# A state-space scan summed by accumulating DMA in SBUF, with three PSUM banks for the side work and one bank for the experts

## The chip, the cores and the metric

The kernel runs on one NeuronCore of a Trainium2 chip. The metric is the device time of one execution in microseconds, as the median of several runs. Everything is fp32; the attention scores use TensorE's fp32r form.

## The reference

Input `x` has 4 images of 128 channels and 64 x 64 pixels, that is L = 4096 tokens each. Two layers follow each other.

Layer 0 normalises, runs a 3 x 3 depthwise convolution with a GELU branch, and then a Mamba block on four groups of 32 channels. The part that matters here is the scan. It has 64 inner channels for each group and N = 16 states:

```
dA  = exp(delta[..., None] * A)                 # A is (64, 16)
dBu = delta[..., None] * Bm[:, :, None, :] * xin[..., None]
h_t = dA_t * h_(t-1) + dBu_t                    # for each channel and state
y_t = sum over n of h_t[:, n] * C_t[n]          # einsum 'bdn,bn->bd'
out = (y + D_skip * xin) * silu(z) @ out_proj_w.T
```

Layer 1 is attention with 4 heads of 32 over all 4096 tokens, softmax without a mask, and then a mixture of 8 experts of 128 x 128: a softmax router, the two largest probabilities renormalised, and `sum over k of p_k * (x @ W_e(k) + b_e(k))`.

## The kernel before, in words

The tokens of an image are cut into 8 blocks of 512. A block of the scan is split into two halves `p` (two of the four channel groups each, 2 x 64 channels = 128 partitions), and the 16 states into 8 pairs. A **unit** is (image b, block i, half p, state pair n): 4 x 8 x 2 x 8 = 512 units. A unit takes two **slots**, so the scan has 1024 slots (`END`). One Python loop over slots writes out all instructions; the `Queue` class makes each engine issue them in exactly that order (so nearly all carry the line of that helper, L467). Nothing reorders them later.

In a slot the loop puts out, in this order: transfers due (`flush`), the fetch of B or C rows for a later unit (`rows`, 512 KB, broadcast from DRAM on SP's queue, four buffers), one decay `da` of the next unit on ScalarE; in the even slot `driven` (h = B row x du) and `scan` on VectorE; in the odd slot `read` (hc = C row x h, 128 x 2 x 512: both states of the pair). One **attention group** goes with each slot when one is ready: two `sc` score tiles on TensorE, two exponentials `pT` on ScalarE, and, one slot later, the products `av` of the group before. Two **lanes**, X and Y, advance by two stages each in every slot. Lane Y makes the inputs of the scan: `first_norm`, `conv`, `inputs`. Lane X closes a block after its scan (`closed`) and does the output projection and experts of finished queries (`finished`), the latter also on lane Y after the scan has ended. Each `yield` in these functions ends a stage. `fetch` calls `until`, which forces the lanes on if a unit's inputs aren't ready.

The sum over the 16 states is on TensorE. Each 128 x 512 product `hc` is transposed in four pieces onto one PSUM bank, in the accumulating mode, for 16 states in turn (`turned_on`); ScalarE copies the bank to `yT`, TensorE turns it back (`turned_back`), and VectorE adds `D_skip * xin` and multiplies with the gate (`scanned`). The list `due` says in which slot a product is taken up, `closing` when a sum is finished. A finished sum also lets lane Y begin the `inputs` that wait for it.

PSUM has eight banks: four for `sc`, one for `av`, one for `y` and one for each lane (`work("X")`, `work("Y")`). The function `inputs` runs in lane Y but also uses lane X's bank, for the gate `pz` and for the B and C rows `pb`.

In `finished`, each pair of experts writes its own accumulation to the lane's bank, and VectorE adds the bank to `res`:

```
            if e:
                vector.tensor_add(res, res, ps)
            vector.tensor_mul(w, w, xf[:, None, :].to_broadcast([P, 2, BLK]))
            yield
            ps = work(lane)
            for u in range(2):
                mm(ps, ew[:, e + u, :], w[:, u, :], u == 0, u == 1)
```

The tile `taps` holds nine diagonal matrices for the convolution of image 0, which runs on TensorE (the other images' convolution runs on VectorE). It lies in the constant pool.

Of the kernel before, what the change touches and what calls it, by code (L numbers as in the profile page):

```python
# [9 lines left out]
F32 = mybir.dt.float32  # L10
# [7 lines left out]
P = 128  # L18
C = 128
# [17 lines left out]
def conv_mamba_attn_moe_kernel(ctx: ExitStack, tc: tile.TileContext, t: dict):  # L37
# [46 lines left out]

    taps = const.tile([P, 9, P], F32, name="taps")
    for k in range(9):
        nc.vector.tensor_scalar_mul(taps[:, k, :], ident, fc1w[:, k : k + 1])
# [385 lines left out]
    def mm(out, lhsT, rhs, start=True, stop=True):  # L473
        tensor.matmul(out, lhsT=lhsT, rhs=rhs, start=start, stop=stop)
# [24 lines left out]
    def pool(name, bufs=1, space=None):  # L499
        return main.enter_context(  # L500
            tc.tile_pool(name=name, bufs=bufs, **({} if space is None else {"space": space}))
        )

    mix, att, side = pool("mix"), pool("att"), pool("side")
    ps_sc, ps_av, ps_y = pool("ps_sc", 2, PSUM), pool("ps_av", 1, PSUM), pool("ps_y", 1, PSUM)
    ps_work = pool("ps_work", 1, PSUM)


    def work(lane, shape=None):
        return ps_work.tile(shape or [P, BLK], F32, tag=f"work{lane}", name=f"ps_{lane}")  # L510
# [132 lines left out]
    def conv(b, i):  # L643
# [4 lines left out]
        def tap(k):  # L648
            y0 = y0_rows(b, i, k // 3, k % 3)
            w = fc1w[:, k : k + 1]  # L650

            if b == 0:
                mm(hr, taps[:, k, :], y0, k == 0, k == 8)
# [59 lines left out]
    def inputs(b, i, p):  # L713
# [3 lines left out]
        while held:  # L717
            yield
            yield
        held.add("in")  # L720
        ps = work("Y")
        summed(ps, [(inxc[:, j, :], pairs[:, p, 2 * j : 2 * j + BLK]) for j in range(2)])
        pz = work("X")
# [8 lines left out]
        pb = work("X")  # L732
# [4 lines left out]
        held.clear()  # L737
# [75 lines left out]
    def read(h, w):  # L813
        hc = mix.tile([P, 2, BLK], F32, name="hc", bufs=2)
        vector.tensor_mul(hc, w, h[:, :, 0:BLK])
        return hc

    def scanned(b, i, p, y):
        xin, zs, delta, du, bcd = in_of.pop((b, i, p))
        vector.scalar_tensor_tensor(xin, xin, dsk, y, ALU.mult, ALU.add)  # L820
        vector.tensor_mul(zs, xin, zs)
        gated[b, i, p] = zs

    def turned_on(y, term, first, last):

        for j in range(NT):
            s = slice(j * P, (j + 1) * P)
            tensor.matmul(
                y[:, s], lhsT=term[:, s], rhs=ident, start=first and j == 0,
                stop=last and j == NT - 1, is_transpose=True,  # L830
            )
# [6 lines left out]

    def turned_back(b, i, p, yT):
        y = ps_y.tile([P, BLK], F32, name="y")  # L840
        for j in range(NT):
            tensor.transpose(y[:, j * P : (j + 1) * P], yT[:, j * P : (j + 1) * P], ident)
        return b, i, p, y
# [243 lines left out]
    def finished(b, qb, lane):  # L1087
# [73 lines left out]

# [23 lines left out]
        ps = work(lane)  # L1185
        mm(ps, eb8, prT[0:NE, :])
        yield
        res = tmp(lane, "res")
        vector.tensor_add(res, ps, xf)
# [3 lines left out]
        yield  # L1193
        for e in range(0, NE, 2):
# [12 lines left out]
        vector.tensor_add(res, res, ps)  # L1207
# [92 lines left out]
    END = 2 * len(units)  # L1300

# [18 lines left out]
    waiting, summing = None, None  # L1320

    while (
        slot < END or due or closing or summing or waiting or left or later or lanes["X"] or running
# [13 lines left out]
        if summing:  # L1337
            summed_up(*summing)
            summing = None
# [6 lines left out]
        if unit and odd:  # L1346
            hc = read(h, rows.pop((at, 1)))
            late = 2 * (unit[3] == 0)
            due.append((slot + 1 + late, unit, 0, hc[:, 0, :], False))
            due.append((slot + 2, unit, 1, hc[:, 1, :], ends(unit)))  # L1350
        advance("Y", False)
        while closing and closing[0][0] <= slot:
            summing = turned_back(*closing.popleft()[1:])
        while due and due[0][0] <= slot:
            _, (b, i, p, n), k, term, done_with = due.popleft()
            first = n == 0 and k == 0
            if first:
                y_of[b, i, p] = ps_y.tile([P, BLK], F32, name="y")
            turned_on(y_of[b, i, p], term, first, done_with)
            if done_with:  # L1360
                yT = mix.tile([P, BLK], F32, name="yT")
                scalar.copy(yT, y_of.pop((b, i, p)))
                closing.append((slot + 1, b, i, p, yT))
# [123 lines left out]
```

## Time and profile before

| | |
|---|---|
| runs shown | 5223.30, 5229.83, 5244.32 us; median 5229.83 us |
| profiled execution, own time | 5221.24 us |
| its span | 5219.4 us |
| PE, PEld busy | 4743.5 us (91%), 2300.7 us (44%) |
| DVE, ACT busy | 3834.5 us (73%), 3749.8 us (72%) |
| POOL busy | 423.5 us (8%) |
| bytes moved by DMA | 1131.62 MB, mean 217 GB/s |
| SP's queue | 1126.74 MB, 64.3% of 16 engines |
| last `hc` product starts | 4608.4 us |

PE is TensorE, PEld its weight loads, DVE VectorE, ACT ScalarE, POOL GpSimd, SP the queue that issues transfers. In the slices, one digit stands for 130.5 us and gives the busy share in tenths. In a row of the groups, the name before `<-` is written and those behind are read; then come the number of instructions, the busy time, the mean duration of one, and the idle time of the engine just before them with what ended it. The profile counts two matmuls for one fp32 call, and one for an fp32r score or a transpose.

### The profile page before, as it was taken

The numbers are of one execution on the slowest core, as the hardware profiler recorded it, in microseconds if no ns is written. First come the engines' busy times: TensorE is split into PE (matmuls) and PEld (weight loads), VectorE is DVE, ScalarE is ACT, GpSimd is POOL, SyncE is SP. The second block draws the span as 40 slices with busy tenths as digits, with TensorE's granted clock in tenths as the row PEclk, the third lists the DMA queues.
The fourth block names the chain that finished last, engine by engine and source line by source line (L and its number), as shares of the span: only waits on it lengthen the run. The fifth ranks groups of instructions, "written<-read, shape, count | busy, mean of one in ns | idle before, by whom it ended". The sixth has DMA issues, their size and how long they took to land.

```text
span 5219.4 us, 62693 instructions
## 1 busy us (share of the span) xinstructions
PE 4743.5 (91%) x20704; PEld 2300.7 (44%) x20704; DVE 3834.5 (73%) x5809; ACT 3749.8 (72%) x5701; POOL 423.5 (8%) x483
## 2 busy tenths in 40 slices
PE   4566898999999999899999999999999999999997
PEld 2333444444444444444444444444444444443443
DVE  4888767777788877888788877888788877751332
ACT  3456787788777777688887787788777787756543
POOL 1111101100000000001000000000000001000000
PEclk8677999999999999899999999999999999999998
DMA  3556667767776667767766667767766666754542
GB/s 96 188 186 202 206 215 247 232 231 238 244 231 218 227 227 243 238 232 246 260 230 231 224 223 230 262 227 259 259 236 227 215 230 226 263 181 153 184 134 72
DMA packets 451694, 1131.62 MB, mean 217 GB/s; under 512 B 51985, under 2 KB 135330, under 8 KB 451362
## 3 DMA queue, kind: packets, MB, share of 16 engines
q1 hardware_dynamic: 450194, 1126.74, 64.3%
q8 instruction: 166, 2.72, 0.2%
q14 instruction: 166, 1.36, 0.1%
q10 hardware_dynamic: 1168, 0.80, 0.1%
HBM read 967.12 MB, written 143.39 MB: 213 GB/s over the span
## 4 chain that ended last, share of the span: by engine, by line
PE 55%; DVE 18%; ACT 13%; DMA 6%; issue 5%; POOL 2%; SPq 1%; DVEq 0%; ACTq 0%; POOLq 0%
PE av L467 23%; PE sc L467 13%; PE ps_X L467 8%; DVE h L467 6%; PE ps_Y L467 5%; PE y L467 5%; ACT pT L467 4%; ACT L467 3%; DMA ks<-kd 2%; DVE hc L467 2%; ACT xt L467 1%; ACT e L467 1%; DMA rows<-bcd 1%; DVE stX L467 1%; POOL rsX L467 1%
## 5 line engine op out<-in xcount | busy, mean ns | idle before, releaser
L467 ACT ACTIVATE pT<-sc 128x1024 f32<-128x1024 f32 x2048 | 1984.8, 1023 | 940.1 <-PE sc L467 938.4
L467 PE MATMUL av<-pT,v 128*64 128x512 f32 x8192 | 1998.3, 609 | 12.4 <-DVE avs L467 12.4
L467 PE MATMUL sc<-qs,ks 128*128 128x512 f32 x4096 | 1296.1, 436 | 64.4 <-DMA ks<-kd 32.7
L467 DVE TENSOR_TENSOR_SCAN h<-da,state,h 128x1025 f32<-128x1025 f32 x512 | 1204.2, 2352 | 90.0 <-ACT h L467 56.2
L467 PEld LDWEIGHTS sc<-qs,ks 128*128 128x128 f32 x4096 | 701.3, 190 | 793.3 <-ACT pT L467 261.7
L467 PEld LDWEIGHTS av<-pT,v 128*64 128x64 f32 x8192 | 499.5, 137 | 844.4 <-issue 813.8
L467 ACT ACTIVATE da<-delta,amat 128x512 f32<-128x512 f32 x1024 | 743.0, 730 | 1.9
L467 PE MATMUL y<-ident,hc 128*128 128x128 f32 x4096 | 626.6, 284 | 64.9 <-DVE hc L467 64.9
L467 DVE TENSOR_TENSOR hc<-rows,h 128x1024 f32<-128x1024 f32 x512 | 624.2, 1219 | 16.1 <-PE y L467 5.9
L467 DVE TENSOR_TENSOR h<-rows,du 128x1024 f32<-128x1024 f32 x512 | 623.4, 1218 | 14.2 <-DMA rows<-bcd 13.7
L467 PEld LDWEIGHTS y<-ident,hc 128*128 128x128 f32 x4096 | 520.6, 147 | 235.7 <-issue 83.9
L467 ACT ACT_TABLE_LOAD x319 | 409.3, 1283 | 19.5 <-DVE zs L467 14.3
L467 POOL TENSOR_TENSOR rsX<-rsX,mhalf 128x4 f32<-128x4 f32 x92 | 203.8, 2216 | 2524.6 <-DVE rsX L467 2440.5
L467 POOL TENSOR_TENSOR rsY<-rsY,mhalf 128x4 f32<-128x4 f32 x100 | 130.4, 1304 | 2071.0 <-DVE shiftY L467 1560.3
L467 DVE TENSOR_TENSOR avs<-av,prev 128x512 f32<-128x512 f32 x96 | 66.1, 689 | 252.9 <-PE av L467 238.3
L467 PE MATMUL ps_X<-share,w_ew 128*128 128x512 f32 x432 | 215.5, 622 | 8.7 <-DVE share L467 8.5
L467 ACT ACTIVATE xt<-ps_Y,shiftY,rsY 128x128 f32<-128x128 f32 x380 | 143.8, 469 | 106.4 <-POOL shiftY L467 99.0
L467 DVE TENSOR_TENSOR share<-share,xf 128x1024 f32<-128x1024 f32 x128 | 155.9, 1218 | 15.6 <-DMA share<-sharesX 9.9
L467 ACT COPY state<-h 128x2 f32<-128x2 f32 x448 | 88.7, 198 | 93.5 <-DVE h L467 93.5
L467 DVE SCALAR_TENSOR_TENSOR cm<-y,w_fc1w,cm 128x512 f32<-128x512 f32 x192 | 142.8, 744 | 3.4
L467 PE MATMUL ps_Y<-pairs,inxc 128*128 128x512 f32 x256 | 129.2, 629 | 15.6 <-DMA pairs<-xn 10.3
L467 PEld LDWEIGHTS ps_X<-share,w_ew 128*128 128x128 f32 x432 | 73.6, 190 | 146.8 <-issue 98.5
(254 smaller groups left out, 3455.8 us busy)
## 6 DMA issues: line engine op xcount, KB each, us to landing
rows<-bcd SPq DMA_DIRECT2D x1024, 512.0 KB
ks<-kd SPq DMA_DIRECT2D x192, 512.0 KB
qs<-qd SPq DMA_DIRECT2D x161, 512.0 KB
share<-sharesX SPq DMA_DIRECT2D x108, 512.0 KB
v<-vd SPq DMA_DIRECT2D x192, 256.0 KB
ks<-kd SPq DMA_DIRECT2D x128, 256.0 KB
avd<-avs SPq DMA_DIRECT2D x96, 256.0 KB
prev<-avd SPq DMA_DIRECT2D x96, 256.0 KB
```

What stands on the lines that cost most here:

```text
L467: return lambda *args, **kw: queued(op(*args, **kw))
```

## The change

1. The two products of a unit are no longer transposed and summed on TensorE. The product of the first pair of states is written to a tile of its own, `sum` (128 x 2 x 512). Each of the other seven pairs is added to it by a transfer within SBUF with an accumulate, issued from GpSimd's queue: 7 x 64 = 448 transfers of 512 KB. VectorE adds the two halves of the tile at the end, in `scanned`. `turned_on`, `turned_back`, `yT` and their bank go.
2. The bank goes to a third work tag, `Z`, that `inputs` uses in place of lane X's bank for `pz` and `pb`. The set `held` is no longer asked.
3. In `finished`, the bias product and all eight experts are accumulated in one bank, and VectorE adds that to `xf` once. Two yields are added ahead of the transposes of `both`.
4. `taps` leaves the constant pool: eight of the nine matrices lie in a buffer of `share`, the ninth in one of `acc`, both used later by `finished`.
5. A finished sum is taken up four slots after the last transfer is issued.

```
-    taps = const.tile([P, 9, P], F32, name="taps")
-    for k in range(9):
-        nc.vector.tensor_scalar_mul(taps[:, k, :], ident, fc1w[:, k : k + 1])
...
-    ps_sc, ps_av, ps_y = pool("ps_sc", 2, PSUM), pool("ps_av", 1, PSUM), pool("ps_y", 1, PSUM)
+    ps_sc, ps_av = pool("ps_sc", 2, PSUM), pool("ps_av", 1, PSUM)
     ps_work = pool("ps_work", 1, PSUM)
+    tap8 = side.tile([P, 2, BLK], F32, name="share", bufs=3).rearrange("p k (j c) -> p (k j) c", c=P)
+    tap9 = side.tile([P, NT, C], F32, name="acc", bufs=2)[:, 0, :]
+    taps = [tap8[:, k, :] for k in range(8)] + [tap9]
+    for k in range(9):
+        vector.tensor_scalar_mul(taps[k], ident, fc1w[:, k : k + 1])
...
-        while held:
-            yield
-            yield
-        held.add("in")
         ps = work("Y")
         summed(ps, [(inxc[:, j, :], pairs[:, p, 2 * j : 2 * j + BLK]) for j in range(2)])
-        pz = work("X")
+        pz = work("Z")
...
-        pb = work("X")
+        pb = work("Z")
         mm(pb[0:DI, :], wbc, xin)
         ps = work("Y")
         mm(ps, wdt, xin)
         yield
-        held.clear()
...
-    def read(h, w):
-        hc = mix.tile([P, 2, BLK], F32, name="hc", bufs=2)
+    def read(unit, h, w):
+        hc = mix.tile([P, 2, BLK], F32, name="hc" if unit[3] else "sum", bufs=2)
         vector.tensor_mul(hc, w, h[:, :, 0:BLK])
         return hc
...
-        vector.scalar_tensor_tensor(xin, xin, dsk, y, ALU.mult, ALU.add)
+        vector.scalar_tensor_tensor(xin, xin, dsk, y[:, 0, :], ALU.mult, ALU.add)
+        vector.tensor_add(xin, xin, y[:, 1, :])
         vector.tensor_mul(zs, xin, zs)
...
(finished)
         yield
-
+        yield
+        yield
         ps = work(lane)
         for j in range(NT):
             tensor.transpose(ps[0 : 2 * NE, j * P : (j + 1) * P], both[:, j, :], ident)
...
-        ps = work(lane)
-        mm(ps, eb8, prT[0:NE, :])
-        yield
-        res = tmp(lane, "res")
-        vector.tensor_add(res, ps, xf)
+        yield
         yield
...
-            if e:
-                vector.tensor_add(res, res, ps)
             vector.tensor_mul(w, w, xf[:, None, :].to_broadcast([P, 2, BLK]))
             yield
-            ps = work(lane)
+            if e == 0:
+                ps = work(lane)
+                mm(ps, eb8, prT[0:NE, :], True, False)
             for u in range(2):
-                mm(ps, ew[:, e + u, :], w[:, u, :], u == 0, u == 1)
-        yield
-        vector.tensor_add(res, res, ps)
+                mm(ps, ew[:, e + u, :], w[:, u, :], False, e + u == NE - 1)
+        yield
+        res = tmp(lane, "res")
+        vector.tensor_add(res, ps, xf)
         send(out[b][:, s], res, 2)
...
(the loop over slots)
-        if summing:
-            summed_up(*summing)
-            summing = None
+        while closing and closing[0][0] <= slot:
+            summed_up(*closing.popleft()[1:])
         advance("X", True)
...
         if unit and odd:
-            hc = read(h, rows.pop((at, 1)))
-            late = 2 * (unit[3] == 0)
-            due.append((slot + 1 + late, unit, 0, hc[:, 0, :], False))
-            due.append((slot + 2, unit, 1, hc[:, 1, :], ends(unit)))
+            hc = read(unit, h, rows.pop((at, 1)))
+            if unit[3] == 0:
+                y_of[unit[:3]] = hc
+            else:
+                due.append((slot + 2, unit, hc))
         advance("Y", False)
-        while closing and closing[0][0] <= slot:
-            summing = turned_back(*closing.popleft()[1:])
         while due and due[0][0] <= slot:
-            _, (b, i, p, n), k, term, done_with = due.popleft()
...
+            _, (b, i, p, n), term = due.popleft()
+            gpsimd.dma_start(out=y_of[b, i, p], in_=term, accum_op=ALU.add)
+            if n == NST - 2:
+                closing.append((slot + 4, b, i, p, y_of.pop((b, i, p))))
         advance("Y", True)
```

More of the change, by code (lines that the diff above doesn't have):

```diff
@@ L652, in tap @@
             if b == 0:
-                mm(hr, taps[:, k, :], y0, k == 0, k == 8)
+                mm(hr, taps[k], y0, k == 0, k == 8)
             elif k == 0:
@@ L819, in scanned @@
         xin, zs, delta, du, bcd = in_of.pop((b, i, p))
-        vector.scalar_tensor_tensor(xin, xin, dsk, y, ALU.mult, ALU.add)
+        vector.scalar_tensor_tensor(xin, xin, dsk, y[:, 0, :], ALU.mult, ALU.add)
+        vector.tensor_add(xin, xin, y[:, 1, :])
         vector.tensor_mul(zs, xin, zs)
         gated[b, i, p] = zs
[L824 to L831, printed above, removed]
     def summed_up(b, i, p, y):
@@ L837, in summed_up @@
             lanes["X"].appendleft((("closed", b, i), closed(b, i), []))
[L839 to L843, printed above, removed]
     vst = side.tile([P, NH, NT, 2 * DH], F32, name="vst")
@@ L1193, in finished @@
         yield
+        ps = None
         for e in range(0, NE, 2):
@@ L1300, in conv_mamba_attn_moe_kernel @@
     END = 2 * len(units)
+    ALONE = NB // 2 * NST
     rows, due, closing, y_of = {}, deque(), deque(), {}
@@ L1318, in ends @@
         return unit[3] == NST - 2
-    waiting, summing = None, None
+    waiting = None
     while (
-        slot < END or due or closing or summing or waiting or left or later or lanes["X"] or running
+        slot < END or due or closing or waiting or left or later or lanes["X"] or running
     ):
@@ L1346, in conv_mamba_attn_moe_kernel @@
         if unit and odd:
-            hc = read(h, rows.pop((at, 1)))
-            late = 2 * (unit[3] == 0)
-            due.append((slot + 1 + late, unit, 0, hc[:, 0, :], False))
-            due.append((slot + 2, unit, 1, hc[:, 1, :], ends(unit)))
+            hc = read(unit, h, rows.pop((at, 1)))
[3 more added lines that the diff above has]
+                due.append((slot + 2, unit, hc))
         advance("Y", False)
-        while closing and closing[0][0] <= slot:
-            summing = turned_back(*closing.popleft()[1:])
         while due and due[0][0] <= slot:
-            _, (b, i, p, n), k, term, done_with = due.popleft()
[L1356 to L1363, printed above, removed]
+            _, (b, i, p, n), term = due.popleft()
+            gpsimd.dma_start(out=y_of[b, i, p], in_=term, accum_op=ALU.add)
+            if n == NST - 2:
+                closing.append((slot + 4, b, i, p, y_of.pop((b, i, p))))
         advance("Y", True)
```

## The prediction

> **What bounds the kernel now.** I read the forty slices first, then the windows, then the chain, then the groups. In the slices (busy tenths) TensorE stands at 9 from about 650 us to the end, VectorE and ScalarE at 7 and 8 until the scan ends at about 4620 us, the DMA engines at 6 and 7, GpSimd near nothing:
>
> ```profile
> PE   4566898999999999899999999999999999999997
> DVE  4888767777788877888788877888788877751332
> ACT  3456787788777777688887787788777787756543
> POOL 1111101100000000001000000000000001000000
> DMA  3556667767776667767766667767766666754542
> ```
>
> The windows turn that into time per slot of the scan. A slot issues four `y<-ident,hc` matmuls, so the number of those counts slots. First all instructions, then, in the second pair, only those on `hc`:
>
> ```profile
> 250.00:500.00 250.00, 156.07 (x593) 88.97 (x591) 213.68 (x274) 134.50 (x257) 28.36 (x28) 0.76 0.59 198
> 1000.00:4250.00 3250.00, 3089.35 (x13892) 1505.44 (x13889) 2634.68 (x3906) 2550.32 (x3907) 271.31 (x318) 0.99 0.70 236
> ...
> 250.00:500.00 250.00, 50.45 (x275) 42.05 (x273) 42.98 (x36) 0.76 0.59 198
> 1000.00:4250.00 3250.00, 420.68 (x2844) 348.98 (x2845) 433.82 (x356) 0.99 0.70 236
> ```
>
> Columns: length, busy time of PE, PEld, DVE, ACT and POOL, clock, DMA share, GB/s; the second pair has only PE, PEld and DVE. From 1000 to 4250 us there are 2844/4 = 711 slots, so **4.57 us a slot**, in which PE is busy 3089/711 = 4.35 us (95%), DVE 3.71 (81%), ACT 3.59 (78%), the DMA engines 0.70 x 4.57 = 3.20 us, moving 236 x 4.57 = 1.08 MB. TensorE sets the slot. The chain of waits agrees where nothing disturbs it: it runs through PE alone.
>
> ```profile
> 2544.48 0.44 PE y L467 x4
> 2544.91 1.87 PE av L467 x8
> 2546.78 1.13 PE sc L467 x4
> 2547.91 0.44 PE y L467 x4
> ```
>
> Of 1024 slots, 450/4 = 112 lie before 500 us (no attention yet, 3.64 us each in the second quarter millisecond, DVE 85% busy). The other **912** lie between 500 and 4620 us: this is the stretch that the change can shorten. From 4620 us on only attention and experts are left, with PE 93% busy; the scan's edits don't touch it.
>
> The groups that I price with (busy us, mean ns):
>
> ```profile
> L467 PE MATMUL y<-ident,hc 128*128 128x128 f32 x4096 | 626.6, 284 | 64.9 <-DVE hc L467 64.9
> L467 PE MATMUL y<-ident,yT 128*128 128x128 f32 x256 | 40.4, 282 | 2.7 <-ACT yT L467 2.7
> L467 ACT COPY yT<-y 128x512 f32<-128x512 f32 x64 | 37.9, 592 | 8.3 <-PE y L467 8.3
> L467 DVE TENSOR_TENSOR res<-res,ps_X 128x512 f32<-128x512 f32 x108 | 73.7, 682 | 51.9 <-PE ps_X L467 51.5
> L467 DVE TENSOR_TENSOR zs<-xin,zs 128x512 f32<-128x512 f32 x64 | 44.3, 692 | 2.2
> ```
>
> **What the Trainium skill says.** "DMA: Bandwidth & Descriptors", SWDGE vs HWDGE vs iDMA: accumulating in a transfer is for GpSimd's queue only, whose cores write the descriptors, and it runs on the same 16 engines as SP's transfers. Before has no such transfer; all its bulk traffic is on SP's queue at 64.3% of 16 engines. The same page, Rules for kernel authors: an accumulate reads its destination and writes it later, so each must wait for the one before on the same bytes. "Collectives: The Full Stack", The bandwidth ceiling: a reducing transfer reads two sources through the same read ring, and goes at half the rate of a copy; no run here shows it. "SBUF — State Buffer", SBUF: two separate sides: GpSimd can be locked out of its port while a DVE instruction holds it; the trace has a sign of that, `rsX` on POOL takes between 1007 and 2978 ns for 128x4.
>
> **The change, part by part.**
>
> *Sum over states: what goes.* 4096 + 256 PE matmuls, 626.6 + 40.4 = 667 us; in the middle 420.7/711 + 0.04 = 0.63 us a slot. PE falls from 4.35 to 3.72. ACT loses 64 copies, 38 us. PE also stops waiting for `hc` (64.9 us in all).
>
> *What the three engines would then allow.* PE 3.72, DVE 3.67 (below), ACT 3.55 are nearly equal. If PE keeps its idle time (4.57 - 4.35 = 0.22) the slot is 3.94; if DVE can't pass the 85% of the start, 3.67/0.85 = 4.32. I take **4.15**, between, and keep 3.94 to 4.32.
>
> *What comes: 448 transfers* (7 for each of 64 sums; the first pair of states is written in place), 7/16 = 0.4375 a slot, 512 KB each. Price P of one in time of all 16 engines: not in the trace. Floor: a copy at the page's ceiling of 435 GB/s, 1.2 us. Above: windows of 6 us in which the DMA share is 0.99 or more show 352 GB/s on average (63 of the 600 between 1000 and 4600 us, from 256 to 414); at that rate a copy takes 1.49 us, and two reads and a write one after another 4.5. I take two reads at 435, an estimate from the Collectives page: **P = 2.4**. The present 1.08 MB a slot at 352 GB/s need 3.06 us. Sum 3.06 + 0.4375 x 2.4 = 4.11 us; if the engines can be kept 95% busy, as PE is now, **4.33 us a slot**. That is more than 4.15: the DMA engines become the bound, and what they leave is 912 x (4.57 - 4.33) = **219 us**. The cover that hid the DMA (3.20 of 4.57) is almost used up.
>
> *The waits it brings.* On POOL each transfer waits for `hc` and for the transfer before it. Behind it stand the `rs` powers and shifts, for which ACT's `xt` waits (already 99.0 + 63.3 us). The transfers come every 16/7 slots, 9.9 us; an estimate is 8 us: about 1 to issue and 2 to land by the DMA page (Anatomy of one DMA), and 2.4 doubled because SP's packets take turns. So the wait is normally over. Descriptors on POOL: 448 x 0.5 to 3 us, against 424 us of work in 5219: covered by an idle engine. On DVE, `hc` must wait for the transfer two units back (four slots, 17 us: covered), and the sum is read four slots after the last transfer. SP issues nothing more, but its `rows` share the engines: they are issued some three slots ahead, 12 to 13 us, and wait now for only 13.7 us in all; this is the wait that I expect to grow.
>
> *The scan's end, two slots later.* Counted from a half-block's first slot, the sum was taken up at slot 19 and now at 21. Lane Y then has 24 slots of stages (3 inputs, 5 first norm, 13 conv, 3 inputs) and meets the fetch in slot 29: done in slot 28 instead of 26, still ahead. The three blocks with a group norm (7 slots more) overrun by two more slots; I put +5 us for forced stages, between 0 and 25.
>
> *DVE.* Experts: of 160 adds of about 686 ns 32 stay, -88 us. The second half of the sum: 64 adds like `zs`, +44 us. Net -44 us, 0.04 a slot, off the DMA-bound path: 0.
>
> *Third bank, later transposes.* PE waits in `ps_X` for `bothX` 45.9, `stX` 23.7, `lo` 20.3 and `zs` 13.8 us: at most -104 us, worth something only while PE sets the slot; with the DMA engines as the bound I count 0. The added two yields lengthen an experts' task by one slot: at most +4 us at the very end, against three to four adds less there: 0. Holding one bank for the whole sum costs nothing while a lane has one task.
>
> *Taps.* The same nine DVE instructions of 279 ns, moved behind the setup, in buffers that nobody else writes before 1366 us: 0, within 3 us either way.
>
> Sum against the profiled execution: 5221 - 219 + 5 = 5007 us. The median of the runs is 9 us above that execution; I forecast **5010**.
>
> **The rivals.**
>
> *Engines set the slot.* Accumulating costs little more than a copy (P under 1.9, where 3.06 + 0.83 over 0.95 is 4.1). For: the reads are from SBUF, and in single windows the DMA reached 414 GB/s. Against: two reads for each write. 5221 - 912 x 0.42 = 4840 us, with 3.94 even 4650.
>
> *The transfers cost more, and the DMA engines set a longer slot.* Place: the 16 engines in the 912 slots, seen as DVE waiting for `rows` and PE for `ks`. It decides from (4.57 x 0.95 - 3.06)/0.4375: **P = 2.93 us**. With P = 3.6, slot (3.06 + 1.58)/0.95 = 4.88: 5221 + 912 x 0.31 = 5504 us, slower. For: windows with the DMA share above 1 that moved only 294 GB/s, so a busy engine isn't a fast one. Against: SBUF reads don't go to HBM.
>
> *The transfers come too late after one another.* They are serial within a sum. It decides from a latency of 16 x 4.57/7 = 10.4 us; at 11 us a slot is 4.81: 5440 us. For: some transfers on the chain take that long (`total<-avs` 11.28 us at 2557 us, among others behind it in the queue). Against: most take about half (`ks<-kd` 5.87 us at 2527 us).
>
> *No change*, gain and loss cancel, P near 2.9: 5225 us.
>
> **How the numbers follow.** DMA engines just full, 5010: 0.33. Engines set the slot, 4840: 0.25. Costly transfers, 5504: 0.26. Late transfers, 5440: 0.09. No change: 0.07. The last counts as within 0.5% (26 us, about what a measurement of this kernel can tell from no change), the two before it as slower: faster 0.58, same 0.07, slower 0.35. The range takes in the engines' case down to a slot of 4.1 (4800) and the costly one up to P = 3.5 (5450). The likeliest case alone, P between 2.0 and 2.8, reaches from 4840 to 5170.
>
> **What would show it.** Right: no `y` group on PE, PE about 86% busy in the middle, a second DMA queue with some 235 MB, DMA share above 0.9 there, slots of 4.3 us, waits for `rows` and `ks` of some 100 us or more. The engines' case: DMA share under 0.85, `pT` and `sc` still the main waits. Costly transfers: the new queue's share over 25%, DMA share near 1, VectorE waiting for `rows`. Late transfers: DVE `hc` or POOL waiting for the accumulating transfer while the DMA share stays low. It would be wrong altogether if the slots before 500 us got longer by more than a tenth: then POOL or the serial chain is slow by itself, without any crowd.

## The result, and the profile after

| | before | after |
|---|---|---|
| runs, median | 5235.17 us (4 runs, 5223.30 to 5244.32; the table ahead of the prediction has three of them) | 5517.71 us (4 runs, 5502.07 to 5524.75) |
| profiled execution, own time, span | 5221.24, 5219.4 us | 5502.07, 5500.2 us |
| mean granted clock of TensorE | 0.958 | 0.900 |

The ratio is 1.0537, with a 95% interval from 1.0502 to 1.0572: the change makes the kernel **5.4% slower**. 5010 us was forecast, with a range up to 5450: it was to become faster, and became slower.

The slices of the kernel after (137.5 us each) and its two bulk queues:

```profile
PE   4344797888788898798888888888888888899997
DVE  4877767777677787877777777777677777751321
ACT  3445686777677777677677777677677777755553
POOL 1221212111111111111111111111121111110000
...
PEclk8566898999999899899999999899899999999998
DMA  3888889898888899999989889989988899974542
...
q1 hardware_dynamic: 450194, 1126.74, 59.8%
q0 software_dynamic: 64512, 234.91, 22.6%
```

TensorE (`PE`), at 9 in before from 650 us on, is at 8 until the scan ends; the DMA engines went from 6 and 7 to 8 and 9. The second queue (`q0`, GpSimd's) moves the expected 235 MB, and takes 22.6% of 16 engines for it, where SP's queue takes 59.8% for 1127 MB: by the byte the new traffic is 1.8 times as dear.

The windows; columns as in the prediction (length, busy time of PE, PEld, DVE, ACT and POOL, clock, DMA share, GB/s):

```profile
250.00:500.00 250.00, 103.83 (x244) 42.55 (x244) 199.44 (x256) 118.86 (x231) 53.40 (x54) 0.62 0.83 231
1000.00:4000.00 3000.00, 2552.60 (x9416) 1040.94 (x9415) 2269.61 (x3340) 2189.38 (x3335) 519.42 (x545) 0.92 0.90 270
```

The same with only the instructions on `rows`, on VectorE. There is one for each slot, so their number counts slots:

```profile
250.00:500.00 250.00, 76.31 (x64) 0.62 0.83 231
1000.00:4000.00 3000.00, 744.02 (x619) 0.92 0.90 270
```

From 1000 to 4000 us there are 619 slots: **4.85 us a slot** against 4.57 before and 4.33 forecast. In a slot PE is busy 4.12 us, DVE 3.67, the DMA engines 0.90 x 4.85 = 4.36.

The early slots, without attention, grew too. Counted the same way, before has 71 of these products in its second quarter millisecond:

```profile
250.00:500.00 250.00, 83.62 (x71) 0.76 0.59 198
```

That is 250/71 = 3.52 us a slot before and 250/64 = 3.91 after. (The 3.64 in the prediction counts transposes, and can't be set against it.) A count of so few is rough, so I also took the starts of VectorE's products `h`, all 512 of which are in both traces. The first 112 slots took 386 us before (98.1 to 483.7) and 419 after (97.6 to 517.0), 9% more; from there to the last `h` it is 4121 us before and 4367 after. The two stretches lost 34 and 246 us, 280 together, and the span grew by 281: the loss lies in the slots of the scan.

The chain that ended last, by engine and by line:

```profile
PE 32%; DMA 30%; DVE 19%; ACT 9%; issue 5%; POOL 2%; SPq 1%; DVEq 0%; POOLq 0%; ACTq 0%
PE av L463 14%; DMA sum<-hc 10%; PE sc L463 8%; DVE h L463 7%; DMA ks<-kd 5%; PE ps_X L463 5%; PE ps_Y L463 4%; DMA inv<-inverse 4%; DMA rows<-bcd 4%; ACT pT L463 3%; ACT L463 2%; DVE hc L463 2%; SPq L463 1%; ACT xt L463 1%; POOL rsX L463 1%
```

DMA is 30% of it, and `sum<-hc`, the new transfer, is its second entry. The groups (busy, mean ns | idle before, what ended most of it) and the DMA issue (KB, median us to landing):

```profile
L463 POOL DMA_DIRECT2D sum<-hc x448 | 395.9, 884 | 2444.6 <-DMA sum<-hc 1501.6
L463 DVE TENSOR_TENSOR hc<-rows,h 128x1024 f32<-128x1024 f32 x448 | 546.7, 1220 | 333.9 <-DMA sum<-hc 274.4
...
sum<-hc POOLq DMA_DIRECT2D x448, 512.0 KB, 8.2
```

The waits (total us, times, longest), three of before ahead of those of after:

```profile
PE sc L467 <- DMA ks<-kd: 32.7, 15, 4.9
DVE aT L467 <- DMA inv<-inverse: 58.9, 18, 9.2
DVE h L467 <- DMA rows<-bcd: 13.7, 9, 2.7
```

```profile
POOL sum L463 <- DMA sum<-hc: 1501.6, 220, 11.2
DVE hc L463 <- DMA sum<-hc: 274.4, 99, 9.6
...
PE sc L463 <- DMA ks<-kd: 195.8, 54, 12.2
...
DVE aT L463 <- DMA inv<-inverse: 154.7, 26, 9.1
...
DVE h L463 <- DMA rows<-bcd: 61.8, 35, 4.3
```

GpSimd waits 1501.6 us for the transfer before; an engine with so little to do can afford that, as long as nobody waits for it. VectorE waits 274.4 us for a free buffer of `hc`, and that was forecast as covered. The wait for `ks` rose from 32.7 to 195.8 us, for `rows` from 13.7 to 61.8, for `inv` from 58.9 to 154.7.

### The profile page after: what moved, and what is told of

It reads as the page before. It is cut to its first block, busy times and chain, and to the rows that moved or that the text cites. A ratio compares the mean times of both kernels' runs of the same rounds, so it can differ in the third digit from the quotient of the medians.

```text
span 5500.2 us, 54845 instructions
## 1 busy us (share of the span) xinstructions
PE 4486.3 (82%) x16352; PEld 1839.6 (33%) x16352; DVE 3800.8 (69%) x5745; ACT 3713.8 (68%) x5637; POOL 876.2 (16%) x931
## 3 DMA queue, kind: packets, MB, share of 16 engines
q1 hardware_dynamic: 450194, 1126.74, 59.8%
q0 software_dynamic: 64512, 234.91, 22.6%
## 4 chain that ended last, share of the span: by engine, by line
PE 32%; DMA 30%; DVE 19%; ACT 9%; issue 5%; POOL 2%; SPq 1%; DVEq 0%; POOLq 0%; ACTq 0%
PE av L463 14%; DMA sum<-hc 10%; PE sc L463 8%; DVE h L463 7%; DMA ks<-kd 5%; PE ps_X L463 5%; PE ps_Y L463 4%; DMA inv<-inverse 4%; DMA rows<-bcd 4%; ACT pT L463 3%; ACT L463 2%; DVE hc L463 2%; SPq L463 1%; ACT xt L463 1%; POOL rsX L463 1%
## 5 line engine op out<-in xcount | busy, mean ns | idle before, releaser
L463 PE MATMUL av<-pT,v 128*64 128x512 f32 x8192 | 2104.2, 637 | 25.7 <-DVE avs L463 23.5
L463 PE MATMUL sc<-qs,ks 128*128 128x512 f32 x4096 | 1357.6, 452 | 321.9 <-DMA ks<-kd 195.8
L463 PEld LDWEIGHTS sc<-qs,ks 128*128 128x128 f32 x4096 | 733.2, 199 | 1106.9 <-ACT pT L463 453.1
L463 PEld LDWEIGHTS av<-pT,v 128*64 128x64 f32 x8192 | 521.4, 143 | 1094.5 <-issue 1015.4
L463 POOL DMA_DIRECT2D sum<-hc x448 | 395.9, 884 | 2444.6 <-DMA sum<-hc 1501.6
L463 DVE TENSOR_TENSOR hc<-rows,h 128x1024 f32<-128x1024 f32 x448 | 546.7, 1220 | 333.9 <-DMA sum<-hc 274.4
L463 DVE TENSOR_TENSOR h<-rows,du 128x1024 f32<-128x1024 f32 x512 | 624.8, 1220 | 69.0 <-DMA rows<-bcd 61.8
L463 ACT ACT_TABLE_LOAD x319 | 409.3, 1283 | 37.7 <-DVE zs L463 32.7
L463 POOL TENSOR_TENSOR rsY<-rsY,mhalf 128x4 f32<-128x4 f32 x100 | 158.5, 1585 | 1067.0 <-DVE shiftY L463 579.7
L463 PE MATMUL ps_X<-share,w_ew 128*128 128x512 f32 x432 | 234.2, 668 | 59.9 <-DVE share L463 59.6
L463 ACT ACTIVATE xt<-ps_Y,shiftY,rsY 128x128 f32<-128x128 f32 x380 | 142.7, 459 | 137.4 <-POOL shiftY L463 130.5
L463 PE MATMUL ps_Y<-pairs,inxc 128*128 128x512 f32 x256 | 143.1, 687 | 48.4 <-DMA pairs<-xn 30.2
L463 PE MATMUL ps_Y<-ident,xt 128*128 128x128 f32 x380 | 75.1, 331 | 120.8 <-ACT xt L463 120.6
```

The source lines that it names most:

```text
L463: return lambda *args, **kw: queued(op(*args, **kw))
```

## The experiments

After the result I had three theories: the load on the 16 DMA engines, the serial chain of seven accumulating transfers, and TensorE itself, slower than counted. The first four experiments turned the second one into another, the place that the transfers have in GpSimd's queue. The change's other parts are a further rival. Before ran beside each group of experiments at a median of 5234 to 5239 us, single runs within 0.25% of their median, so differences under some 25 us are not read. The kernels in the table ran once each, except after. Times of kernels that leave out or alter work are no times of a complete kernel.

| kernel | time, us | slot, us | DMA share 1000-4000 us |
|---|---|---|---|
| after | 5517.71 | 4.85 | 0.90 |
| no transfers | 5098.15 | 4.43 | 0.71 |
| plain copies | 5234.13 | 4.60 | 0.82 |
| half of the rows' bytes | 5326.54 | 4.66 | 0.80 |
| issued at once | 5347.16 | 4.72 | 0.92 |
| issued at once, plain copies | 5172.38 | 4.49 | 0.84 |
| issued at once, half of the rows' bytes | 5170.35 | 4.50 | 0.82 |
| before, with a light sum | 5113.31 | 4.44 | 0.71 |
| no transfers, no `hc` products | 5007.35 | 4.37 | 0.72 |

### What the transfers cost: none, copies, fewer other bytes

No transfers:

```
-            gpsimd.dma_start(out=y_of[b, i, p], in_=term, accum_op=ALU.add)
```

> The changed kernel with its 448 accumulating transfers left out: the sum keeps only the first pair of states, every other instruction stays. Theory A (the transfers fill the 16 DMA engines; 2.77 us of them each, 22.6% of the span): without them the DMA share in the middle falls from 0.90 to about 0.70, the slot from 4.8 us to the 4.15 us that I put for the compute engines, the time to about 4900 us. Theory B (the transfers of one sum come one after another, 8.2 us each from issue to landing, and hold up POOL's queue and VectorE's hc): the same fall, 4900 us. Theory C (TensorE's granted clock is lower because it has less to do, 0.90 against 0.96, and the rest of its work takes longer): the clock stays near 0.9 or falls, and the time stays above 5100 us.

Plain copies instead of accumulating ones:

```
-            gpsimd.dma_start(out=y_of[b, i, p], in_=term, accum_op=ALU.add)
+            gpsimd.dma_start(out=y_of[b, i, p], in_=term)
```

> The changed kernel with the same 448 transfers of 512 KB on the same queue with the same order and waits, but as plain copies (the sum is overwritten, not added to). Theory A: a copy needs about half of an accumulate's engine time, 1.2 to 1.5 us for 2.77, the DMA share in the middle falls from 0.90 to about 0.80, the time to about 5150 us. Theory B: the time goes with the latency from issue to landing; if that falls from 8.2 to 5 us, also about 5150; if it stays above 7.5, no change, 5500. If accumulating costs the engines no more than copying, the share of the queue stays 22% and the time 5500 us.

Only one state's row is fetched, 256 KB instead of 512:

```
-            out=w.rearrange("p m q -> p (m q)"),
+            out=w[:, 0, :],
...
-        return w
+        return w[:, 0:1, :].to_broadcast([P, 2, BLK])
```

> The changed kernel with the B and C rows of one state of each pair only (256 KB a transfer in place of 512 KB, the second state uses the first one's rows); the accumulating transfers stay as they are. Theory A: SP's queue loses 268 MB of 1127, the DMA share in the middle falls from 0.90 to about 0.75, waits for ks, rows and inv go back to what they were before the change, and the time falls to about 5000 us. Theory B: the chain of accumulates stays, its latency falls only as far as the crowd thins (8.2 to 7 us); the time falls by under 150 us, to 5350 or more.

Measured: 5098.15, 5234.13 and 5326.54 us. No theory had all of this. Without transfers the time falls far less than to 4900; theory C, with its lower clock (0.92 here), is the nearest. The copy brings 284 us where theory A had 350. With half of the rows' bytes the time lies between the 5000 of one theory and the 5350 of the other. The windows of the kernel without transfers:

```profile
1000.00:4000.00 3000.00, 2732.82 (x10349) 1111.12 (x10349) 2484.98 (x3666) 2402.67 (x3672) 295.76 (x297) 0.95 0.71 243
```

In 677 slots of 4.43 us PE is busy 4.04 us and the DMA engines 0.71 x 4.43 = 3.15. So the transfers cost 5518 - 5098 = 420 us, but all that their absence brings against before is 137 us, where the forecast's engines' slot of 4.15 would have brought 380. The copies' page:

```profile
q1 hardware_dynamic: 450194, 1126.74, 63.8%
q0 software_dynamic: 64512, 234.91, 11.3%
...
sum<-hc POOLq DMA_DIRECT2D x448, 512.0 KB, 6.4
```

The same 235 MB take 11.3% of 16 engines, 1.32 us for each transfer; accumulating takes 22.6% x 5500.2 / 448 = **2.775 us**. The ratio is 2.1. "Collectives: The Full Stack" of the Trainium skill, The bandwidth ceiling, says of ReduceScatter, in which several cores add up their data, that its transfers read two sources through one read ring and so go at half the rate of copies: these runs agree, for a sum within the SBUF of one core. Fewer other bytes give 191 us back, so the sum of bytes matters, and not the new transfers alone.

### Where the transfer stands in GpSimd's queue

The timeline of POOL in after (start, duration, instruction, [idle time before, what ended it]):

```profile
2535.04 0.86 POOL L463 DMA_DIRECT2D sum<-hc  x1 [9.29 <-DMA sum<-hc]
2559.79 1.94 POOL L463 TENSOR_TENSOR rsX<-rsX,mhalf 128x4 f32<-128x4 f32 x1 [23.89 <-DVE rsX L463]
2561.70 0.90 POOL L463 DMA_DIRECT2D sum<-hc  x1
2569.75 1.13 POOL L463 DMA_DIRECT2D sum<-hc  x1 [7.14 <-DMA sum<-hc]
```

and of DVE, the `hc` products around it:

```profile
2541.49 1.23 DVE L463 TENSOR_TENSOR hc<-rows,h 128x1024 f32<-128x1024 f32 x1
...
2559.61 1.22 DVE L463 TENSOR_TENSOR hc<-rows,h 128x1024 f32<-128x1024 f32 x1
...
2569.23 1.23 DVE L463 TENSOR_TENSOR hc<-rows,h 128x1024 f32<-128x1024 f32 x1 [0.64 <-DMA sum<-hc]
```

The product that starts at 2541.49 is done at 2542.72. Its transfer goes out at 2561.70, **19 us later**: in POOL's queue it stands behind `rsX`, which waits until 2559.79 for statistics from VectorE. The transfer then takes 7.5 us, and the next but one `hc`, which needs the same buffer, waits for it until 2569.23. Between 600 and 4600 us 363 transfers can be set against their products in order: the mean delay from the end of the product to the issue is 7.7 us, the longest 19.7, and for 77 of them it is over 10.

So the transfer was put into the queue in the slot of its product, ahead of what the lanes issue in the next two slots, with the end of the sum where it was:

```
-                due.append((slot + 2, unit, hc))
+                due.append((slot, unit, hc))
...
-                closing.append((slot + 4, b, i, p, y_of.pop((b, i, p))))
+                closing.append((slot + 6, b, i, p, y_of.pop((b, i, p))))
```

> The changed kernel with each transfer put on POOL's queue right behind its hc (same slot), not two slots later behind the rs powers of those slots; the sum is still taken up in the same slot. Bytes and their order on the engines stay. Theory A (load of the DMA engines): no change, 5480 to 5540 us. Theory B, now narrower (a transfer stands behind rs powers that wait for VectorE, goes out late, lands 8 us later, and VectorE's next but one hc waits for its buffer, 274 us in all): that wait falls under 120 us and the time by about 150, to 5350 us.

Measured: 5347.16 us, 171 us less than after, as theory B had it. The mean delay fell to 1.9 us, with one over 10. Its groups:

```profile
L463 POOL DMA_DIRECT2D sum<-hc x448 | 394.0, 879 | 2725.9 <-DVE hc L463 1195.4
...
L463 DVE TENSOR_TENSOR hc<-rows,h 128x1024 f32<-128x1024 f32 x448 | 546.0, 1219 | 29.6 <-DMA rows<-bcd 15.1
```

`hc` waits 29.6 us in all (333.9 in after), 7.9 of them for transfers. GpSimd itself now waits longer, mostly for `hc`, and 977.4 us of its waits still are for the transfer before: the serial chain is there as it was, and hardly anything waits for it. But 4.72 us a slot is still above before's 4.57, at the highest DMA share of all:

```profile
1000.00:4000.00 3000.00, 2615.24 (x9734) 1062.42 (x9732) 2344.18 (x3464) 2264.61 (x3453) 554.33 (x566) 0.93 0.92 278
```

What is left shows in the waits for SP's loads. From the kernel without transfers to this one, PE's wait for `ks` rises from 57.6 to 175.6 us, and VectorE's for `rows` (into `h`) from 16.1 to 78.7, for `inv` from 105.4 to 158.2 and for `share` rows of lane X from 36.7 to 93.5.

### The two causes together

Issued at once, and plain copies:

> Plain copies in place of accumulates, and each put on the queue right behind its hc: the two edits of e2 and e5 together. If load and place in the queue are two separate losses (270 us for the second read, 160 us for the place), the gains add up partly: 5130 to 5180 us, near the 5098 without transfers. If they are one loss, seen twice, 5230.

Issued at once, and half of the rows' bytes:

> Accumulating transfers put on the queue right behind their hc, and half the bytes of the B and C rows (the second state of a pair uses the first one's): the edits of e3 and e5 together. If what e5 leaves (5347 against 5098 without transfers) is the load of the DMA engines, then 5120 to 5180 us, since the share falls from 0.92 to about 0.80. If it is the latency of a single transfer, over 5250 us.

Measured: 5172.38 and 5170.35 us, both within what was expected. Two quite different ways to take load from the DMA engines, the accumulate's second read or half of the rows' bytes, give the same 175 and 177 us once the place in the queue is mended, and bring their share down to 0.84 and 0.82. What is left above the kernel without transfers is 74 and 72 us. So of the 420 us, taken off in this order, about 170 are the place in the queue, 175 the accumulate's extra load, and 75 the rest of the transfers. The first two are not independent: with late transfers the copy saves 284 us, because a shorter transfer also shortens the lateness.

### Buffers and the serial chain

A third buffer for `hc` needs room, which a third buffer of `share` gives up. The control gives that up alone:

```
-                w = side.tile([P, 2, BLK], F32, name="share", bufs=3)
+                w = side.tile([P, 2, BLK], F32, name="share", bufs=2)
```

> A control for the next two, which need 4 KB of SBUF a partition: the changed kernel with two buffers of share (512 KB rows of the experts' shares, and the taps) in place of three. No theory speaks of it; experts take 5% of the stages, so 5500 to 5560 us, and what the next two gain or lose is counted from here.

With the third `hc` buffer:

```
-        hc = mix.tile([P, 2, BLK], F32, name="hc" if unit[3] else "sum", bufs=2)
+        hc = mix.tile([P, 2, BLK], F32, name="hc" if unit[3] else "sum", bufs=3 if unit[3] else 2)
```

> The control with three buffers of hc in place of two, so that VectorE's product waits for the transfer three units back and not two. Theory A: the time stays within 30 us of the control. Theory B: DVE's wait for sum<-hc (274 us) falls under 60 us and the time by 150 to 250 us.

Both, and issued at once:

> Transfers at once, three buffers of hc, two of share (the edits of e5 and e7 together). The place in the queue and the missing buffer are one wait (VectorE's hc for a transfer that went out late): with the place mended the third buffer brings little, 5347 + 48 for the share buffer less 0 to 40, so 5355 to 5395 us. If they are separate, 5300.

Measured: 5565.13 for the control, just above what was expected, 5471.34 with the third buffer, 5434.38 with it and the early issue. The third buffer brings 94 us, less than expected, although `hc` then waits 32.5 us in all; one part of the reason is that the end of a sum (`xin`) now waits 50.6 us for its last transfer, 8.1 in the control. With the early issue the third buffer brings nothing: the two remove the same wait. 5434 is even more than the 5347 plus the control's 47 us, and more than expected; VectorE's wait for `share` rows rose from 93.5 to 159.1 us.

Two sums for each half-block, so that a transfer needn't wait for the one before it (not shown: `sum` gets three buffers, where two sums of a half-block in turn with two of the next would need four, and VectorE adds four halves at the end in place of two):

```
-            gpsimd.dma_start(out=y_of[b, i, p], in_=term, accum_op=ALU.add)
+            gpsimd.dma_start(out=y_of[b, i, p][n // 2 % 2], in_=term, accum_op=ALU.add)
...
-                closing.append((slot + 4, b, i, p, y_of.pop((b, i, p))))
+                closing.append((slot + 2, b, i, p, y_of.pop((b, i, p))))
```

> The control with two sums for each half-block, even and odd pairs of states, so that a transfer follows the one two units back and not the last one: 6 transfers in place of 7, two more adds of 0.69 us at the end, and the sum taken up two slots earlier. Theory A: the load falls by a seventh of the transfers, the DMA share by 3 points, the time by about 50 us. Theory B in its first form (serial order within a sum): POOL's wait for the transfer before (1502 us) falls under 500 us and the time by 150 us or more from the control.

Measured: 5696.02 us, 131 above the control. Its waits:

```profile
POOL sum L463 <- DVE hc L463: 1656.4, 231, 19.0
...
PE sc L463 <- DMA ks<-kd: 308.4, 79, 19.5
DVE hi L463 <- PE ps_X L463: 244.2, 38, 14.2
...
DVE hc L463 <- DMA sum<-hc: 57.7, 26, 6.9
```

GpSimd's wait is now for `hc`, not for the transfer before, and there are 64 transfers fewer (384); `hc` waits 57.7 us for transfers instead of 251.2 in the control. The time rose all the same, against both theories. By itself this run doesn't clear the serial order, since it changes more than that: it ends its sums two slots earlier, with fewer buffers for each, and has 128 more adds on VectorE. The waits for `ks` (308.4 against 231.8 in the control), `ps_X` into `hi` (244.2 against 70.4) and, at the end of a sum, for its transfers (73.2 against 8.1) grew; which of these changes is to blame stays open. The early issue says more: there the serial chain stayed, and the waits of `hc` for transfers went.

### The same sum by GpSimd instead of transfers

```
-            gpsimd.dma_start(out=y_of[b, i, p], in_=term, accum_op=ALU.add)
+            gpsimd.tensor_add(y_of[b, i, p], y_of[b, i, p], term)
```

> The changed kernel with each of the 448 transfers replaced by one add of 128x1024 on GpSimd itself (sum + hc, both in SBUF), at the same place in its queue: no bytes on the DMA engines. By the Trainium skill (GPSIMD Engine Reference, Elementwise, 4497 ns for 2048 elements) an estimate is 2.25 us each, 1.0 us a slot on an engine that is busy 0.4. If the adds run beside VectorE: the slot of the run without transfers, 4.4 us, so 5100 to 5150 us, which beats both kernels. If the port that GpSimd shares with VectorE is held for whole instructions: VectorE gets 448 x 2.25 = 1000 us of blocking on 3.7 us a slot, 5500 to 6000 us.

Measured: 5412.3 us (5401 to 5416), ratio to before 1.033, from 1.0312 to 1.0347, between the two ranges and nearer to the second. The DMA engines are back at 0.68. The additions (duration in ns: least, median, longest):

```profile
L463 POOL TENSOR_TENSOR sum<-sum,hc x448: 2337/2743/4412, 112.0 to 4810.0; 128x1024 f32<-128x1024 f32 x150
```

and on VectorE at the same time:

```profile
L463 DVE TENSOR_TENSOR h<-rows,du x512: 1159/1219/3397, 98.6 to 4802.9; 128x1024 f32<-128x1024 f32 x171
L463 DVE TENSOR_TENSOR_SCAN h<-da,state,h x512: 2340/2356/4447, 99.9 to 4804.3; 128x1025 f32<-128x1025 f32 x171
```

In after the longest `h` product is 1259 ns and the longest scan 2367. Here they reach 3397 and 4447, 2.1 us more, a little less than the shortest addition. "SBUF — State Buffer" of the Trainium skill, SBUF: two separate sides, states it: a VectorE instruction with two SBUF inputs and a GpSimd instruction that reads SBUF take the shared ports in turn, each for a whole instruction. These lines agree. DVE is busy 4493.8 us instead of 3800.8. So the sum is off the DMA engines and on VectorE, by way of the ports.

### TensorE without the transposes

Before, with the sum over states of the first pair alone; all else (two banks, its sum's end, its experts) stays:

```
+            light = (n, k) in ((0, 0), (0, 1))
...
-            turned_on(y_of[b, i, p], term, first, done_with)
+            if light:
+                turned_on(y_of[b, i, p], term, first, k == 1)
```

> The kernel before with TensorE's sum cut to the first pair of states (512 of 4096 transposes stay, the sum leaves out the other states); banks, lanes, experts and the end of the scan as before. It asks whether the 5098 us of the changed kernel without transfers come from the arrangement (third bank, later end of a half-block, two more yields) or from the other engines' work. If the arrangement is neutral: 5098 + 0.09 us of PE a slot, 5100 to 5150 us. If the arrangement costs: under 5070. If the third bank gains: over 5170.

After without transfers, and without the 448 products:

```
-            hc = read(unit, h, rows.pop((at, 1)))
+            w1 = rows.pop((at, 1))
+            hc = read(unit, h, w1) if unit[3] == 0 else None
...
-            gpsimd.dma_start(out=y_of[b, i, p], in_=term, accum_op=ALU.add)
```

> The changed kernel without transfers and without the 448 products hc that they would have added (only the first pair of states is read out): VectorE loses 448 x 1.22 = 546 us, 0.53 us a slot of its 3.67. It asks what sets the slot of 4.43 us without transfers. If TensorE with its lower clock does (4.04 us busy a slot): it can't go under 4.04/0.95 = 4.25, so 4930 us or more. If VectorE's order does: by most of the 0.53 us, 4620 to 4750 us. Half way: both take turns, and a slot is the sum over stages of whichever is later.

Measured: 5113.31 and 5007.35 us, the first as for a neutral arrangement, the second as where VectorE does not hold the slot. The windows of the first,

```profile
1000.00:4000.00 3000.00, 2722.86 (x10832) 1156.96 (x10830) 2494.63 (x3696) 2421.25 (x3711) 257.77 (x301) 0.97 0.71 243
```

and of the second:

```profile
1000.00:4000.00 3000.00, 2764.22 (x10498) 1128.96 (x10500) 2181.47 (x3422) 2440.32 (x3735) 292.54 (x302) 0.95 0.72 247
```

The first has 4.44 us a slot, the kernel without transfers 4.43: taking the transposes away yields the same in the old arrangement as in the new. In the second VectorE does 0.53 us a slot less, and only 0.06 us is gained: VectorE's work is not what holds the slot at 4.4. PE is busy 4.02 us a slot there, 92%, at a granted clock of 0.95.

The waits of PE without transfers, beside those of before, say where part of its time goes:

```profile
PE sc L467 <- ACT pT L467: 30.5, 91, 1.6
PE ps_Y L467 <- ACT xt L467: 71.3, 22, 7.7
```

```profile
PE sc L463 <- ACT pT L463: 131.5, 135, 3.1
PE ps_Y L463 <- ACT xt L463: 121.5, 56, 10.5
```

The waits that grew most end with ScalarE: the scores wait for the exponentials that free their PSUM banks. ScalarE is busy 2402.67/677 = 3.55 us of the 4.43. So without the transposes TensorE gives a good part of its time back as waits for ScalarE. No run takes work off ScalarE, so it isn't shown that this sets the slot.

### The experts alone

The new `finished` in before:

```
-            ps = work(lane)
+            if e == 0:
+                ps = work(lane)
+                mm(ps, eb8, prT[0:NE, :], True, False)
             for u in range(2):
-                mm(ps, ew[:, e + u, :], w[:, u, :], u == 0, u == 1)
+                mm(ps, ew[:, e + u, :], w[:, u, :], False, e + u == NE - 1)
```

> The kernel before with the experts' part of the change alone (bias and eight experts in one PSUM bank, two more yields); scan, lanes' banks and taps as before. All theories put the loss in the transfers, so this must not be slower than before. It takes 128 adds of 0.69 us (88 us) off VectorE, which is 81% busy beside a TensorE at 95%, and PE's waits for bothX (46 us) off the path: 5180 to 5235 us against 5235. If it is slower by more than 0.5%, part of the loss lies in the experts.

Measured: 5241.97 us, ratio 1.0011, from 1.0003 to 1.002: 80 us of adds fewer on VectorE (3755.3 us busy), and nothing for it, where up to 55 us were expected.

## Why the prediction was wrong, point by point

**The frame held.** No `y` group is left on PE, the second queue moves 235 MB, the share of the DMA engines is 0.90, the wait for `ks` is over 100 us and that for `rows` 61.8. PE is 85% busy where 86% was forecast, but by luck: 4.12 of 4.85 us and not 3.72 of 4.33. The early slots grew by 9% (11% by the count in one window), at the very edge of the tenth that was to refute the frame; the crowd was there too, with a DMA share of 0.83 against 0.59, and without transfers they are as short as before (72 in the window). The experts were counted at 0, and are. The third bank, the shifted transposes and the taps weren't tried one by one; the slots of the light sum in before and of after without transfers, 4.44 and 4.43 us, suggest that they count for little.

**"PE falls from 4.35 to 3.72": the first step that failed.** It is 4.04 without transfers. The traces show why. Busy time of PE by tile in a slot, before (658 slots from 1000 to 4000 us) and without transfers (677):

| us a slot | before | no transfers |
|---|---|---|
| `y` | 0.63 | 0 |
| `av` | 1.90 | 2.02 |
| `sc` | 1.24 | 1.27 |
| `ps_X`, `ps_Y`, `ps_Z` | 1.04 | 1.07 |
| their overlap | -0.47 | -0.31 |
| PE busy | 4.33 | 4.04 |
| PE idle | 0.23 | 0.39 |

Of the 0.63, 0.16 lay beside other matmuls and was no time of PE's at all. (The ends of matmuls are modelled in the profile, so this share is rough.) The chain of before had it in plain sight: four transposes are 0.44 us there. Another 0.17 comes back because the remaining matmuls take longer. The median `av` is unchanged at 592 ns and the longest is 1117, about twice that, while the mean of the group went from 609 to 633 and the granted clock from 0.98 to 0.95 between 1000 and 4000 us. In that stretch 0.8% of the `av` took over 900 ns before, and 7.2% without transfers: more of them ran at half rate. "TensorE: Matmul & The Clock Gate" of the Trainium skill, Part 1, says that the clock has two states, full when TensorE has been busy and half after it has been idle; the two durations agree. So a TensorE with gaps is also slower, which the sum left out. And **"if PE keeps its idle time (0.22)"** failed as well: the idle time rose to 0.39, with ScalarE at the end of the waits that grew most. 4.04 + 0.39 = 4.43, above even the 4.32 that was kept as the upper end. The gain to be had was 137 us, a third of what the engines' slot of 4.15 promised, before any transfer was paid.

**"P = 2.4": 2.775 us.** The factor of two held and the copy was mis-sized, 1.32 where the ceiling of 435 GB/s gave 1.2. (In the Trainium skill that ceiling stands in "DMA: Bandwidth & Descriptors", Where 436 GB/s comes from; "Collectives" has the factor alone.) **"The present 1.08 MB a slot need 3.06": 3.15**, as the share of the kernel without transfers shows; 3.20 stood in before's own windows, and I had replaced it by a rate from selected windows. Together the DMA engines need 3.15 + 0.4375 x 2.775 = 4.36 us where I had 4.11. Over 0.95 that is 4.59, already no gain. This moves the point from which the costly transfers decide from 2.93 to (4.34 - 3.15)/0.4375 = 2.72, under what was measured.

**"If the engines can be kept 95% busy": 0.92 at best.** At 0.92 much the same need, 4.34 us, takes 4.72, the slot of the kernel with early issue. 0.95 was TensorE's own share in before, and I had carried it over to the DMA engines with no view to support it; the slices of before show no stretch at that share. The prediction also took the larger of two slots, the compute engines' and the DMA engines'. The runs show no such switch: at a DMA share of 0.82 to 0.84 the slot is 4.49 to 4.50, still above the 4.43 without transfers. The waits for `ks`, `rows`, `inv` and `share` grow together; which of them withholds the rest isn't shown.

**"So the wait is normally over" and "four slots, 17 us: covered".** The landing was close to the estimate (8.2 us against 8), in part by luck: the 2 us that I took from "Anatomy of one DMA" hold the setup too, by that section's table, so the 1 us for the issue was counted twice. An issue takes 0.85 to 1.14 us, within the 0.5 to 3 that I had allowed. What failed was to count the landing from the product: GpSimd's queue adds 7.7 us on average and up to 19.7. I had named `rs` and the shifts as standing behind the transfers, and not asked what the transfers stand behind. The wait that I named did not grow by the transfers: `xt` waits 130.5 + 103.8 us for the shifts after, and 129.3 + 102.9 without transfers. The late issue brings the slot from 4.72 to 4.85.

**The sum, with measured terms.** From the 4.33 forecast to the measured 4.85, 0.26 us are the need of the DMA engines (4.59), 0.13 their share (4.72) and 0.13 the late issue. 912 x (4.85 - 4.33) = 474 us above 5007, and 34 us for the early slots, which I had left at nothing: 5515 against 5502.

**The rivals.** "Costly transfers" gave 5504 with P = 3.6, close by number and not by its size, since P is 2.775. "Late transfers" decided from a latency of 10.4 us; the landing took 8.2, the lateness came from the queue ahead of it, and two chains didn't help. "Engines set the slot", at 4.15, is excluded by the kernel without transfers. None had its whole mechanism right: a slightly dearer transfer, in a late place, for a smaller prize.

No complete version of the changed sum that was tried beats before: issued at once it is 5347 us, with GpSimd's additions 5412.

## What to carry to other kernels

Price removed work by what the chain of waits loses, not by its busy time, and allow for the clock that TensorE loses with its gaps and for the waits that come up behind it: here 0.63 us of busy time were 0.44 on the chain and 0.14 of the slot. A transfer moved to another engine's queue is late by whatever that queue waits for ahead of it: list both what stands behind it and what it stands behind, and issue it as soon as its data is due. When a move fills another resource to nine tenths, size that resource from its share of the present slot, with the new term measured, since errors of a tenth decide the sign.

## What the runs showed of the hardware that I had not expected

- Accumulating 512 KB within SBUF takes 2.775 us of 16 engines and lands 8.2 us after issue (median; least 4.4); the copy takes 1.32 and 6.4 (least 2.8). The landing is three to five times the engines' own time.
- Issuing one costs GpSimd 0.85 to 1.14 us, a copy 0.55 on average, beside a VectorE that is busy 69% of the time: no sign of the lock-out from the port that I had feared for the issue. GpSimd's additions do show it, on both sides.
- TensorE's granted clock falls with few gaps: from 1000 to 4000 us 0.98 at 95% busy (before), 0.95 at 91% (no transfers), 0.92 at 85% (after). The busy share alone doesn't set it: with the light sum it is 0.97 at 91%.
